# A four-layer graph network: the norm, ranks and feed-forward products of layer 0 inside its attention pass, and the end loops of layers 1 and 3 joined

## The chip, the cores and the metric

One core of a Trainium2 chip runs the whole network in one launch. Times are device microseconds. The time of the kernel before is the median of three runs; its profile comes from one further execution that the hardware profiler recorded. TensorE is called PE (PEld for its weight loads), VectorE DVE, ScalarE ACT, GpSimd POOL, and the queue that issues most plain DMAs SP.

## The reference, cut to what matters

N = 3750 nodes of 256 features, 60000 edges sorted by destination, where destinations are drawn as 3750 u² and so crowd at low node numbers. Eight blocks are added to a residual stream, each on a layer-normed copy:

```python
x = x + L0_gnn(layernorm(x)); x = x + L0_ffn(layernorm(x))   # and so for layers 1, 2, 3
# L0_gnn: relational graph attention, 4 heads, softmax over the edges of each destination
e     = leaky_relu(el[src, type] + er[dst, type], 0.2)
alpha = exp(e - segment_max(e, dst)[dst]);  alpha /= segment_sum(alpha, dst)[dst]
h     = segment_sum(alpha * feat[type, src], dst) + h_bias
# L0_ffn on the normed x: only the N//2 - 1 nodes with the largest router weight get the product
w     = x @ wr + br
sel   = top_k(w, N // 2)[: N // 2 - 1]
out   = x;  out[sel] += w[sel] * (gelu(x[sel] @ w1 + b1) @ w2 + b2)
# L1_ffn: two of 8 experts, chosen from the mean over all nodes
out   = layernorm(sum_of_two_experts(x) + x) * gamma + beta
# L3_ffn: each node goes to two of 16 experts
out   = layernorm(x + moe(x)) * gamma + beta
```

Layers 1 and 2 have attention over the same edges, layer 3 two hypergraph convolutions; layer 2's feed-forward sends each node to one of 8 experts.

## The kernel before

Nodes lie on 128 partitions in NT = 30 tiles, and `self.x` keeps all of them in SBUF. Edges are cut into chunks of 128; each chunk belongs to one destination tile. The list `CAPS` says how many chunks a tile gets (90 for tile 0, 38 for tile 1, down to 10, and 3 for the last), 525 with padding.

**The attention pass** (`Regular.attention`) is one function for layers 0, 1 and 2. It handles GC = 7 chunks as a group, 75 groups in all, and, with 4 heads, NG = 4 groups as a batch for the softmax. Per group g:
- `fetch` issues seven indirect DMA gathers on POOL (L135) into a buffer `gt` of the pool `atg` (9 buffers);
- `choose` makes the transposed one-hot `ohT` of the destinations on ACT (L1780, L1781) and multiplies it on PE into the destination's logit part (`er_ps`, L931);
- `make_logits` adds both parts on DVE (L938 to L943); once a batch, `softmax_1` and `softmax_2` turn logits into weights (DVE scans, an Exp on ACT, transposes on PE);
- four groups later `onehot` makes the one-hot `oh` on ACT (L1789, L1791), `scale_rows` multiplies the gathered rows on DVE (L1897) and copies the weights beside them on ACT (L1898), and `sums` has PE add them up into `sum_ps` (L1915);
- `add` moves finished sums to an accumulator for all tiles, on ACT (L1934) for a tile's first piece and on DVE (L1939, L1940) for those that join.

The pass runs under a manual schedule: on DVE, PE, ACT and POOL the order is that of the Python code. Elsewhere a planner orders the instructions by priority and its own costs. [...]

**Around it.** `l01` runs `l0_gnn`, `l0_ffn`, `l1_gnn`, `l1_ffn`. Behind the gathers of layer 0 it puts 320, and behind those of layer 1 another 160, indirect scatters on POOL (L141): they write a table that later layers read. A memset on DVE at the end of the pass (`behind`) holds them back until the last gathers are out.

`l0_gnn` ends with a loop over the 30 tiles (L952 to L955) that divides, adds the bias and adds to `self.x`. `l0_ffn` then takes statistics of all tiles, transposes all normed tiles to `xT_all`, computes the router row for all nodes (L1014, L1015), and ranks each node against all others: per tile two long compare-and-count operations on DVE over the nodes before it and after it (L1029, L1032). Only with all ranks there do the products start, three tiles at a time: 8 hidden products with Gelu (L1047, L1049), then 24 matmuls for the outputs (L132), then three DVE operations a tile. `l1_gnn` begins with statistics of `self.x` and per tile a product that writes the table its gathers read.

`l1_ffn` has the same loop of threes, keeps all outputs in `f1_y`, and then `add_normed` (L977 to L979) normalises the 30 tiles and adds them to `self.x`; `l2_gnn` takes statistics of `self.x` again. `l3_ffn` runs 74 chunks through their experts, then for each tile norms `self.x` (L118), adds the expert bias (L1759), gathers its two rows by POOL and adds them (L1763), and after all tiles calls `add_normed`; `store` writes the result at the very end.

Of the kernel before, what the change touches and what calls it, by code (L numbers as in the profile page):

```python
# [10 lines left out]
F32 = mybir.dt.float32  # L11
# [10 lines left out]
P = 128  # L22
# [36 lines left out]
class Gnn:  # L59
# [55 lines left out]

    def normed(self, out, src, stats, t):
        mv, rstd = stats
        self.nc.vector.tensor_scalar(out, src[:, t, :], mv[:, t, 0:1], rstd[:, t:t + 1],  # L118
                                     op0=ALU.subtract, op1=ALU.mult)
# [64 lines left out]
    def store(self):  # L184
        nc, out = self.nc, self.out
        for a in range(0, NT - 1, 10):
            b = min(a + 10, NT - 1)
            nc.sync.dma_start(out[a * P:b * P].rearrange("(t p) d -> p t d", p=P), self.x[:, a:b, :])
        nc.sync.dma_start(out[(NT - 1) * P:N], self.x[:NLAST, NT - 1, :])
# [799 lines left out]
    def l0_ffn(self):  # L989
# [3 lines left out]
        with ExitStack() as st:  # L993
# [10 lines left out]
            wm = pool.tile([P, NT], F32, name="f0_wm")  # L1004
            with ExitStack() as st2:
                rp, wp, pp = self.pools(st2, f0r=1, f0rw=2, f0rp=-2)

                wrb = rp.tile([P, 2, P], F32, name="wrb")
                nc.vector.tensor_copy(wrb, wr.to_broadcast([P, 2, P]))
                row = rp.tile([P, NP], F32, name="wrow")  # L1010
                for c0 in range(0, NP, 480):
                    ps = pp.tile([P, 480], F32, name="wr_ps")
# [3 lines left out]
                nc.vector.memset(row[:, N:], -3.0e38)  # L1016

                col = rp.tile([P, NT], F32, name="wcol")
                parts = rp.tile([P, NT, 4], F32, name="rank_parts")
                nc.vector.memset(parts, 0.0)  # L1020
                for t in range(NT):
                    own = row[:, t * P:(t + 1) * P]
                    mask = wp.tile([P, P], F32, name="mask")
                    nc.vector.tensor_tensor(mask, own, self.ident, ALU.mult)
                    nc.vector.tensor_reduce(col[:, t:t + 1], mask, AX.X, ALU.add)
                    w = col[:, t:t + 1]
                    junk = wp.tile([P, NP], F32, name="junk")
                    if t:
                        nc.vector.tensor_scalar(junk[:, :t * P], row[:, :t * P], w, None, op0=ALU.is_ge,  # L1029
                                                op1=ALU.add, accum_out=parts[:, t, 0:1])  # L1030
                    if t < NT - 1:
                        nc.vector.tensor_scalar(junk[:, (t + 1) * P:], row[:, (t + 1) * P:], w, None,  # L1032
                                                op0=ALU.is_gt, op1=ALU.add, accum_out=parts[:, t, 1:2])
                    nc.vector.tensor_scalar(mask, own, w, None, op0=ALU.is_gt, op1=ALU.add,
                                            accum_out=parts[:, t, 2:3])
                    nc.vector.scalar_tensor_tensor(mask, own, w, self.after, op0=ALU.is_equal, op1=ALU.mult,
                                                   accum_out=parts[:, t, 3:4])
                rank = rp.tile([P, NT], F32, name="rank")
                nc.vector.tensor_reduce(rank, parts, AX.X, ALU.add)
                nc.vector.scalar_tensor_tensor(wm, rank, float(KEEP), col, op0=ALU.is_lt, op1=ALU.mult)  # L1040
            wp, pp, yp = self.pools(st, f0w=2, f0p=-3, f0y=-3)
            for t0 in range(0, NT, T):
                hT = wp.tile([P, FC, T * P], F32, name="hT")
                for f in range(FC):
# [4 lines left out]
                    nc.scalar.activation(hT[:, f, :], ps, AF.Gelu_apprx_tanh, bias=b1[:, f:f + 1], scale=1.0)  # L1049
                for t in range(t0, t0 + T):  # L1050
# [716 lines left out]
class Regular(Gnn):  # L1767
# [26 lines left out]
    def attention(self, acc, table, idx, row, W, H, select, logits, with_max=False):  # L1794
# [7 lines left out]
        with ExitStack() as st:  # L1802
# [102 lines left out]
            def sums(g, oh):  # L1905
# [3 lines left out]
                for j in range(GC):  # L1909
# [6 lines left out]
                    if starts(k + 1):  # L1916
                        ready.append(open_)
# [344 lines left out]
```

## Time and profile before

| | us |
|---|---|
| median of three runs | 6599.66 (6581.83 to 6659.76) |
| the profiled execution | 5979.16 |
| its span | 5977.2 |
| layer 0's first gather | 371.3 |
| layer 0's last gather, start | 1031.6 |
| layer 0's ranks (DVE) | 1141 to 1284 |
| layer 0's products (PE) | 1288 to 1494 |
| layer 1's first gather | 1563.4 |
| layer 1's products (PE) | 2355 to 2564 |
| layer 2's first products | 2620.9 |
| layer 3's rows gathered | 5840 to 5915 |
| last DVE operation | 5968 |

Over the span PE is busy 75%, PEld 55%, DVE 51%, ACT 34%, POOL 49%; the mean granted PE clock is 0.828. Numbers such as 0.95 are a duration in us; in the timeline a row is: start, duration, engine, line, operation, output and input, how many merged, and in brackets the idle time before it and what ended it. In the table of waits a row is: who waited, for whom, total us, times, longest.

### The profile page before, as it was taken

What the parts mean: (1) busy time and instruction counts of PE and PEld (TensorE: products, weight loads), DVE (VectorE), ACT (ScalarE), POOL (GpSimd) and SP (SyncE); (2) the same over time, 40 slices, a digit from 0 to 9 for tenths busy, and PEclk for the clock granted to TensorE, in tenths of its full rate; (3) what the DMA queues carried; (4) which work ended last, traced back from release to release, by engine and by line L of the source; (5) the groups of instructions that cost most, each with busy time, mean ns of one, the idle gap of its engine ahead of it and who ended that gap; (6) DMA issues with size and microseconds to landing.
All of it is one profiled execution on the core that took longest, in us unless ns stands there. A gap on an engine that the chain in (4) does not pass through costs nothing.

```text
span 5977.2 us, 64725 instructions
## 1 busy us (share of the span) xinstructions
PE 4455.3 (75%) x20324; PEld 3263.5 (55%) x20438; DVE 3077.3 (51%) x7318; ACT 2042.3 (34%) x4826; POOL 2912.3 (49%) x2845
## 2 busy tenths in 40 slices
PE   5937777239577774967877835997799999995993
PEld 2426666127456652734666623774466666664781
DVE  5454544862343347255888886006533433565336
ACT  1225665112366662213555532223531211110220
POOL 0047777877677778604666610102055546540113
PEclk9967787669777786988888865995599999997995
DMA  4335555100455542015777722223445545554122
GB/s 145 135 112 139 139 141 124 22 1 2 112 140 140 140 116 45 2 53 186 229 222 224 224 79 77 92 74 115 156 150 167 144 128 172 151 127 134 55 56 83
DMA packets 427052, 710.10 MB, mean 119 GB/s; under 512 B 117180, under 2 KB 304516, under 8 KB 422604
## 3 DMA queue, kind: packets, MB, share of 16 engines
q0 software_dynamic: 145136, 379.81, 24.6%
q1 hardware_dynamic: 262952, 312.54, 16.4%
q10 hardware_dynamic: 18612, 13.50, 0.8%
q8 instruction: 166, 2.72, 0.2%
q14 instruction: 186, 1.52, 0.1%
HBM read 579.88 MB, written 125.15 MB: 118 GB/s over the span
## 4 chain that ended last, share of the span: by engine, by line
PE 45%; DVE 14%; issue 6%; DMA 6%; POOL 6%; ACT 3%; DVEq 0%; ACTq 0%; SPq 0%; POOLq 0%
PE third_ps L2136 7%; PE sum_ps L1915 6%; PE y_ps L132 6%; POOL gt L135 5%; PE two_ps L2134 4%; PE hT_ps L1735 3%; PE db_psT L2048 2%; PE y_ps L1744 2%; PE h_ps L1530 2%; PE q_ps L1286 2%; DMA gt<-l_vk,srci 2%; PE qkvs_ps L132 2%; PE h_ps L1232 2%; PE h_ps L1047 2%; DMA gt<-l_h,srci 2%
## 5 line engine op out<-in xcount | busy, mean ns | idle before, releaser
L1915 PE MATMUL sum_ps<-gt,oh 128*128 128x260 f32 (+2 forms) x3150 | 1002.0, 484 | 269.1 <-ACT gt L1898 156.6
L1915 PEld LDWEIGHTS sum_ps<-gt,oh 128*128 128x128 f32 x3150 | 755.5, 246 | 446.3 <-ACT gt L1898 164.6
L135 POOL DMA_INDIRECT gt<-l_vk,srci x525 | 497.9, 948 | 452.8 <-DVE hd_hc L687 231.1
L141 POOL DMA_INDIRECT blocks<-put x480 | 639.7, 1333 | 154.0 <-issue 145.6
L135 POOL DMA_INDIRECT gt<-l_feat,g x525 | 501.5, 955 | 172.8 <-issue 149.0
L135 POOL DMA_INDIRECT gt<-l_h,srci x525 | 496.9, 946 | 178.6 <-issue 138.9
L1789 ACT ACTIVATE oh<-iota,dloc 128x128 f32<-128x128 f32 x1575 | 481.2, 386 | 3.8 <-PE sum_ps L1915 3.8
L1897 DVE TENSOR_TENSOR gt<-gt,bank 128x1792 f32<-128x1792 f32 x225 | 453.5, 2016 | 42.9 <-PE bank L1926 40.0
L135 POOL DMA_INDIRECT gt<-l_mtab,l_idxm x300 | 297.1, 990 | 308.8 <-ACT gt L2120 160.3
L135 POOL DMA_INDIRECT gt<-l_xtab,srci x262 | 254.2, 970 | 321.5 <-DMA l_xtab<-xt 191.9
L132 PE MATMUL y_ps<-f_w,hT 128*128 128x256 f32 x1600 | 351.7, 380 | 0.0
L2134 PE MATMUL two_ps<-l_twom,slab 128*128 128x512 bf16 x1020 | 341.9, 379 | 0.0
L2134 PEld LDWEIGHTS <-slab 128*128 128x128 bf16 x2160 | 211.2, 98 | 235.9 <-issue 0.4
L2134 PE MATMUL two_ps<-l_twox,slab 128*128 128x512 bf16 x1026 | 338.7, 379 | 0.1
L132 PEld LDWEIGHTS y_ps<-f_w,hT 128*128 128x128 f32 x1600 | 304.3, 190 | 46.5
L2136 PE MATMUL third_ps<-l_thirdm,slab 128*128 128x257 bf16 x1080 | 294.8, 273 | 3.2
L2136 PE MATMUL third_ps<-l_thirdx,slab 128*128 128x257 bf16 x1080 | 293.2, 273 | 3.0
L1780 ACT ACTIVATE ohT<-rows,iota_p 128x896 f32<-128x896 bf16 x225 | 235.3, 1046 | 120.6 <-DMA rows<-dl_dram 64.4
L2136 PE MATMUL third_ps<-gt,oh 128*128 128x257 f32 x1124 | 266.3, 382 | 3.3 <-DMA gt<-l_xtab,srci 3.3
L1286 PE MATMUL q_ps<-l_qt,ohT 128*128 128x256 f32 x1050 | 248.8, 390 | 20.1 <-DVE gt L1292 11.9
L125 PE MATMUL xT_ps<-ident,xn 128*128 128x128 f32 x360 | 64.0, 296 | 261.5 <-DVE xn L118 138.4
L1781 ACT ACTIVATE ohT<-ohT,ones 128x896 f32<-128x896 f32 x225 | 234.4, 1042 | 7.3
(541 smaller groups left out, 8463.7 us busy)
## 6 DMA issues: line engine op xcount, KB each, us to landing
rows<-dl_dram SPq DMA_DIRECT2D x225, 224.0 KB
slab<-adT SPq DMA_DIRECT2D x36, 960.0 KB
slab<-ad SPq DMA_DIRECT2D x30, 1152.0 KB
l_feat<-ft SPq DMA_DIRECT2D x30, 1040.0 KB
f_w<-in_L_ffn_w_dram SPq DMA_DIRECT2D x18, 1024.0 KB
adT<-db_rowT SPq DMA_DIRECT2D x36, 480.0 KB
ad<-db_row SPq DMA_DIRECT2D x36, 480.0 KB
f_yt<-y SPq DMA_DIRECT2D x114, 128.0 KB
```

The source lines that it names most:

```text
L132: self.nc.tensor.matmul(ps, xT[:, c, :], w[:, c, :], start=(c == 0), stop=(c == kc - 1))
L135: return self.nc.gpsimd.indirect_dma_start(out=out, out_offset=None, in_=table, in_offset=bass.IndirectOffsetOnAxis(ap=idx, axis=0))
L141: inst = self.nc.gpsimd.indirect_dma_start(out=table, out_offset=bass.IndirectOffsetOnAxis(ap=idx, axis=0), in_=src, in_offset=None)
L1286: nc.tensor.matmul(ps[:, j, :], ohT[:, j * P:(j + 1) * P], flat(q[:, ds(tiles[j], 1), :]), start=True, stop=True)
L1735: nc.tensor.matmul(ps[:, f, :], mine[:, c, f * P:(f + 1) * P], xT[:, c, :], start=(c == 0), stop=(c == 1))
L1780: nc.scalar.activation(t, rows, AF.Abs, bias=self.iota_p, scale=-1.0)
L1781: nc.scalar.activation(t, t, AF.Relu, bias=self.ones[:, 0:1], scale=-1.0)
L1789: nc.scalar.activation(oh[:, j, :], self.iota, AF.Abs, bias=self.dloc[:, c + j:c + j + 1], scale=-1.0)
L1897: nc.vector.tensor_tensor(rows, rows, wj.unsqueeze(3).to_broadcast([P, GC, H, DH]), ALU.mult)
L1915: nc.tensor.matmul(open_[1], oh[:, j, :], gt[:, j, :W], start=starts(k), stop=starts(k + 1))
L2134: nc.tensor.matmul(flat(ps), block, flat(two[n][:, blocks[i][1]]), start=(i == 0), stop=(i == len(blocks) - 1))
L2136: nc.tensor.matmul(ps3[:, :D + 1], block, rhs, start=(i == 0), stop=(i == len(all3) - 1))
```

## The change

**Layer 0.** `l0_gnn` and `l0_ffn` of the regular path become one function, `l0`. `attention` gets two hooks: `done(t, sums)`, called from `add` when tile t has all its sums, which are then taken straight from PSUM or from a small buffer `ring` and no longer kept for all tiles; and `steps(n)`, called twice in each iteration, before `softmax_2` and after `sums`. `done` divides, adds, and takes the statistics of the tile; each pair of tiles then goes through three queues of small pieces. `steps` takes one piece of `nodes` (norm, transpose, router row) per call, one of `ranks` in every fourth call, and one (first call) or two (second) of `products`: 8 hidden products of 256 columns and 4 half outputs per pair. Ranks compare a tile with the tiles before it only; the reverse counts come from matmuls of the bf16 comparison with a column of ones. Outputs go to DRAM unweighted, and after the pass they are read back and added with weight or zero. What is left in the queues is worked off after the pass, behind the issue of the scatters. The pass has 8 gather buffers for 9 and three sum banks for four; products share one PSUM bank `hbank`, router and transposes another, er and the reverse counts a third.

**Layers 1 and 3.** Statistics of `self.x` are taken tile by tile where it is last written. `l1_ffn` norms and adds in its loop of three tiles. `l3_ffn` reads the normed rows from DRAM, where they already are, adds `beta` to `self.x` beside the expert products, and norms, adds and stores three tiles at a time. (The irregular path, which these inputs don't take, has its ranks moved into its product loop.)

```diff
@@ Regular.attention
             def add():
-                k, ps = ready.pop(0)
+                nonlocal ring
+                k, ps, end = ready.pop(0)
                 t = TILE_OF[k]
...
+                last = end == len(TILE_OF) or not joins(end)
+                if joins(k):
+                    out = acc[:, t, :] if done is None else ring
...
+                elif done is None or not last:
+                    out = ring = acc[:, t, :] if done is None else wp.tile([P, W], F32, name="ring")
+                    nc.scalar.copy(out, ps)
+                else:
+                    out = ps
+                if done is not None and last:
+                    done(t, out)
...
                 elif g + 1 == ALL and self.behind is not None:
                     self.behind()
+                steps(0)
                 if new:
                     softmax_2(full)
...
                     sums(k, oh)
+                steps(1)
                 while g >= ALL + NG and ready:
                     add()
@@ Regular.l0
+                def done(t, sums):
...
+                    self.row_stats(mv, bn, self.x, t)
+                    if t % T == T - 1:
+                        two = slice(t + 1 - T, t + 1)
+                        nc.scalar.activation(rstd[:, two], mv[:, two, 1], AF.Sqrt, bias=self.eps, scale=1.0)
+                        nodes.append((norm, t + 1 - T))
+
+                def norm(t0):
+                    nc.vector.reciprocal(rstd[:, t0:t0 + T], rstd[:, t0:t0 + T])
+                    xT = wp.tile([P, 2, T * P], F32, name="xT")
+                    then = []
+                    for i in range(T):
+                        xn = wp.tile([P, D], F32, name="xn")
+                        self.normed(xn, self.x, (mv, rstd), t0 + i)
+                        nc.vector.tensor_tensor(self.x[:, t0 + i, :], self.x[:, t0 + i, :], xn, ALU.add)
+                        then.append((turn, t0 + i, xn, xT))
+                    nodes[:0] = then + [(weigh, t0 + i, xT) for i in range(T)]
+
+                def turn(t, xn, xT):
+                    ps = ybank[:, t % 2 * D:][:, :D].rearrange("p (c n) -> p c n", c=2)
+                    for c in range(2):
+                        nc.tensor.transpose(ps[:, c, :], xn[:, c * P:(c + 1) * P], self.ident)
+                    nc.scalar.copy(xT[:, :, t % T * P:(t % T + 1) * P], ps)
+                    if t % T == T - 1:
+                        products.extend((hidden, xT, f) for f in range(FC))
+                        products.extend((outer, t + 1 - T + i, c) for i in range(T) for c in range(2))
...
+                def compare(t):
...
+                    for i, lo in enumerate(range(0, t * P, HALF)):
+                        hi = min(lo + HALF, t * P)
+                        nc.vector.tensor_scalar(ge[:, :hi - lo], row[:, lo:hi], w, None, op0=ALU.is_ge,
+                                                op1=ALU.add, accum_out=rank[:, t, 2 + i:3 + i])
+                        a, b = lo // P, hi // P
+                        ps = ebank[:, 2 * GC * RH + 32:2 * GC * RH + 32 + b - a]
+                        for u in range(a, b):
+                            nc.tensor.matmul(ps[:, u - a:u - a + 1], ge[:, (u - a) * P:(u - a + 1) * P], one,
+                                             start=True, stop=True)
+                        nc.vector.tensor_tensor(less[:, a:b], less[:, a:b], ps, ALU.add)
+
+                def hidden(xT, f):
...
+                    ps = hbank[:, f % 2 * T * P:(f % 2 + 1) * T * P]
+                    for c in range(2):
+                        nc.tensor.matmul(ps, w1[:, c, f * P:(f + 1) * P], xT[:, c, :], start=(c == 0), stop=(c == 1))
+                    nc.scalar.activation(hT[:, f, :], ps, AF.Gelu_apprx_tanh, bias=b1[:, f:f + 1], scale=1.0)
+
+                def outer(t, c):
+                    ps = hbank[:, t % 2 * D:][:, :D]
+                    for f in range(c * FC // 2, (c + 1) * FC // 2):
+                        nc.tensor.matmul(ps, hT[:, f, t % T * P:(t % T + 1) * P], w2[:, f, :],
+                                         start=(f == 0), stop=(f == FC - 1))
+                    if c:
+                        y = wp.tile([P, D], F32, name="y")
+                        nc.vector.tensor_tensor(y, ps, b2, ALU.add)
+                        nc.sync.dma_start(ydram[t * P:(t + 1) * P], y)
+
+                def do(queue):
+                    if queue and not (queue is nodes and queue[0][0] is norm and len(products) > 2 * T + FC):
+                        f, *args = queue.pop(0)
+                        f(*args)
+
+                def steps(n):
+                    do(nodes)
+                    if next(every):
+                        do(ranks)
+                    for _ in range(1 + n):
+                        do(products)
+                self.attention(None, self.feat, g0, D + H, D + H, H, select, logits, bufs=8, sums_bufs=3,
+                               done=done, steps=steps)
+            behind()
+            while nodes or ranks or products:
+                for queue in (nodes, ranks, products, products):
+                    do(queue)
...
+            for t0 in range(0, NT, G):
+                y = gp.tile([P, G, D], F32, name="f0_got")
+                nc.sync.dma_start(y, ydram[t0 * P:(t0 + G) * P].rearrange("(t p) d -> p t d", p=P))
+                for t in range(t0, t0 + G):
+                    nc.vector.scalar_tensor_tensor(self.x[:, t, :], y[:, t - t0, :], wm[:, t:t + 1], self.x[:, t, :],
+                                                   op0=ALU.mult, op1=ALU.add)
+                    bn = wp.tile([P, 6], F32, name="bn")
+                    self.row_stats(xmv, bn, self.x, t)
@@ l1_ffn
-                        nc.vector.tensor_tensor(y[:, t, :], xn, ps, ALU.add)
-            self.add_normed(pool, y, "L1_ffn_gamma", "L1_ffn_beta", "f1n")
+                        nc.vector.tensor_tensor(y[:, t - t0, :], xn, ps, ALU.add)
+                        self.row_stats(ymv, bn, y, t - t0)
+                    self.inverse_std(yr, ymv)
+                    for t in range(t0, t0 + T):
+                        row, x = y[:, t - t0, :], self.x[:, t, :]
+                        nc.vector.tensor_tensor(x, x, beta, ALU.add)
+                        nc.vector.scalar_tensor_tensor(row, row, ymv[:, t - t0, 0:1], gamma, op0=ALU.subtract, op1=ALU.mult)
+                        nc.vector.scalar_tensor_tensor(x, row, yr[:, t - t0:t - t0 + 1], x, op0=ALU.mult, op1=ALU.add)
+                        self.row_stats(mv, bn, self.x, t)
@@ l3_ffn
-            self.add_normed(yp, y, "L3_ffn_gamma", "L3_ffn_beta", "f3n")
...
+            for t0 in range(0, NT, T):
+                y = wp.tile([P, T, D], F32, name="f3_yall")
+                nc.sync.dma_start(y, xtab[t0 * P:(t0 + T) * P].rearrange("(t p) d -> p t d", p=P))
...
+                        nc.vector.scalar_tensor_tensor(row, r, wts[i][:, t:t + 1], row, op0=ALU.mult, op1=ALU.add)
+                    bn = wp.tile([P, 6], F32, name="bn")
+                    self.row_stats(mv, bn, y, t - t0)
+                self.inverse_std(rstd, mv)
+                for t in range(t0, t0 + T):
+                    row, x = y[:, t - t0, :], self.x[:, t, :]
+                    nc.vector.scalar_tensor_tensor(row, row, mv[:, t - t0, 0:1], gamma, op0=ALU.subtract, op1=ALU.mult)
+                    nc.vector.scalar_tensor_tensor(x, row, rstd[:, t - t0:t - t0 + 1], x, op0=ALU.mult, op1=ALU.add)
+                self.store(t0, t0 + T)
```

## The prediction

> **What bounds the kernel now.** I split the span into stages first (stretches with each engine's busy time, in this order: us, then PE, PEld, DVE, ACT, POOL with instruction counts, granted clock, DMA share, GB/s):
>
> ```profile
> 371.00:1032.00 661.00, 466.03 (x2126) 396.96 (x2127) 315.53 (x687) 392.76 (x847) 501.02 (x525) 0.77 0.55 138
> ...
> 1141.00:1288.00 147.00, 3.78 (x12) 1.90 (x10) 145.94 (x252) 1.77 (x3) 116.84 (x100) 0.52 0.08 1
> 1288.00:1494.00 206.00, 205.86 (x788) 151.09 (x788) 49.45 (x115) 45.80 (x80) 163.87 (x139) 0.98 0.08 2
> ...
> 2565.00:2621.00 56.00, 1.21 (x5) 0.84 (x5) 54.80 (x190) 1.18 (x4) 0.00 (x0) 0.52 0.10 28
> ...
> 5915.00:5977.00 62.00, 0.00 (x0) 0.00 (x0) 53.38 (x184) 0.32 (x1) 0.04 (x1) 0.50 0.20 65
> ```
>
> The first is layer 0's attention pass, then layer 0's ranks (DVE alone) and its feed-forward products (PE alone); the fourth is layer 1's normalisation after its products and the last the end of layer 3 (DVE alone in both). At first sight the 353 us of rows two and three are what the change could hide. The POOL timeline says otherwise:
>
> ```profile
> 1031.56 0.95 POOL L135 DMA_INDIRECT gt<-l_feat,g  x1 [0.30 <-issue]
> 1037.13 1.24 POOL L1997 DMA_DIRECT2D put<-put_dram  x1 [4.62 <-DVE put L1995]
> 1043.22 1.25 POOL L141 DMA_INDIRECT blocks<-put  x1 [4.86 <-DMA put<-put_dram]
> ...
> 1073.48 26.20 POOL L141 DMA_INDIRECT blocks<-put  x1 [0.30 <-issue]
> ...
> 1563.40 0.99 POOL L135 DMA_INDIRECT gt<-l_h,srci  x1 [18.95 <-ACT ohT L1780]
> ```
>
> POOL issues its last layer-0 gather at 1031.6, then 320 scatters until 1544.5, and layer 1's first gather at 1563.4. So ranks and products lie beside scatters that layer 1's gathers queue behind anyway: only 19 us separate the two. In the pass POOL is the bound: a gather every 1.25 us, 7 x 1.25 = 8.75 us per group. Who waits in the pass (us 450 to 1000; total, times, longest), and below it ACT's own timeline:
>
> ```profile
> DVE l L942 <- DMA gt<-l_feat,g: 192.6, 57, 6.5
> POOL gt L135 <- issue: 124.0, 407, 0.3
> ```
>
> ```profile
> 827.88 1.04 ACT L1780 ACTIVATE ohT<-rows,iota_p 128x896 f32<-128x896 bf16 x1
> 828.96 1.04 ACT L1781 ACTIVATE ohT<-ohT,ones 128x896 f32<-128x896 f32 x1
> 829.90 2.14 ACT L1789 ACTIVATE oh<-iota,dloc 128x128 f32<-128x128 f32 x7
> 832.07 1.04 ACT L1791 ACTIVATE oh<-oh,ones 128x896 f32<-128x896 f32 x1
> ...
> 848.34 0.16 ACT L1898 COPY gt<-bank 128x28 f32<-128x28 f32 x1
> ...
> 853.83 0.16 ACT L1898 COPY gt<-bank 128x28 f32<-128x28 f32 x1
> ```
>
> Everything waits for gathers, POOL for nothing. Where gathers are already there, one group's copy (L1898) follows the last by 5.5 us, which is ACT's own work: the compute side has 3.2 us to spare per group, but in a fixed order.
>
> [...]14 sum records take 3.31 us at 821.6 and 5.95 us at 848.6. [...] The trace has loads of 1.28[...].
>
> **Layer 0's pass, part by part.** Removed behind it: finishing (31 us), statistics, transposes, ranks (147), products (206). Added inside: per pair of tiles 5 node steps, 2 comparisons, 8 hidden products, 4 outer ones. Prices: 24 matmuls of 256 columns take 10.36 us (L132), 0.43 each, so a hidden product h is 0.86 and half an outer one o 1.73. A Gelu over 256 columns g: between 0.37 (128 columns, L1741) and 0.58 (384, L1049), I take 0.45. Two transposes 0.5 and their copy 0.37 (L125, L126). Sums s 3.1, er products r 1.65, ohT 2.08, oh 3.2, copy 0.18.
>
> Totals would fit: on DVE a tile adds about 6.3 us (three adds 1.0, bn 0.4, norm and add 0.7, comparison about 1.0 plus 2.3 for the long one, the rest 0.9), 3 us a group beside 315/75 = 4.2. On PE 8 x 0.86 + 4 x 1.73 = 13.8 us a pair. The order doesn't fit. In an iteration ACT does ohT, the Gelu of the product in steps(0), oh, the copy, and then the Gelus of steps(1); these wait for products that PE does after the sums, which wait for the copy. Behind the waiting Gelus stand the next ohT and oh; for them wait er, its logits, and the next sums. So from copy to copy is a closed chain through PE and ACT, which the kernel before doesn't have. By kind of iteration, as the queues fall out when CAPS is worked through (4 iterations a pair once saturated):
> - outer, then turn: s + 2o + r + 0.5 + 0.37 + oh + copy = 12.4
> - turn, then hidden: s + 0.5 + 0.37 + 2h + g + ohT + r + h + g + oh + copy = 14.6
> - hidden, then hidden: the same without the turn, 13.7
> - hidden, then outer: s + 2h + g + ohT + (r + o) + copy = 10.9
>
> Mean 12.9. [...] Rank matmuls, one per earlier tile, some 14 on average by then at the 98 ns of a bf16 weight load (L2134), in every second iteration: 0.7. Table loads between Exp, Gelu and Sqrt mostly fall into ACT's waits, as the one at 393.7 did (Exp followed only at 423.2): 0.1, from 0 up to 1.3 (four in four iterations). Sum 14.3, or 5.55 above POOL's 8.75.
>
> Tiles end late: 90, 38, 30 chunks first, 10 to 15 at the end. Pairs 0 to 2 make bursts (iterations 24 to 41) worth 4, 4.5 and 4 such iterations; from 42 on every one carries products, and POOL's last fetch needs iteration 70: 29. Lag: 22 minus three free iterations that catch up 3.25 each gives 12; plus 25 minus one free one is 34; plus 22 is 56; plus 29 x 5.55 = 161 is 217. POOL's 8 buffers let it stay 3 iterations (26 us) ahead. The last gather is **191 us later**. Bounds: 0 below, since POOL's 1.25 us per gather is untouched and excludes a gain; above, with PE at half clock throughout, the 8 us of PE work in a mean chain (s, r, h, o, transposes) double in 29 + 14 iterations: 191 + 43 x 8 = 535. I take warm PE.
>
> Then the 320 scatters, 320 x 1.484 = 475, 12 before them[...]: layer 1's first gather comes 497 us after the last of layer 0, not 532: **-35**. What remains (10 iterations 143, some 40 products 50, the combine from DRAM 30 x 0.8 = 24 and its loads, layer 1's node products 62) is 290 us and hidden; without scatters it would be the next bound. Layer 1's first statistics (17) vanish there too, worth nothing. SP: 2.1 MB of weights go ahead of the pass's first rows, seg and ends loads; at the 224 GB/s of layer 2's pass 9 us, caught up before iteration 24. The y stores and reloads (3.9 MB each way) meet DMA at a 0.55 share: nothing. toh in bf16: nothing. Three sum banks for four: POOL-bound groups leave them free; 0 to 10, I take 0.
>
> **Layer 1.** Products end at 2564.4, the next layer's first at 2620.9. What remains of it: last tile's add and statistics 1, Sqrt with a load 1.6, three tiles x (add 0.34, two at 0.40, bn 0.39) 4.6, statistics over all tiles 1, norm and transpose 2; per block two table loads on ACT can hold PE (three banks of 1.29 us against 2.9 us of loads and Sqrt) by up to 0.8, ten times 8. 2564 + 10 + 8 = 2583: **-38** (0 to -50). DVE's extra 3.4 us per tile fits: it is busy 51 of the products' 210 us now.
>
> **Layer 3.** POOL's 60 gathers (5840 to 5915) stay. DVE per tile: add 0.34, four fused ones at 0.40, bn 0.39 = 2.35, under POOL's 2.5. After the last gather lands, 5918, some 6 us of arithmetic and the store, 8 as now: 5932 for 5977: **-45**, say -44[...]. The beta adds go beside expert products (DVE busy 157 of 400 us there): nothing.
>
> **Sum.** 191 - 35 - 38 - 44 = +74. The profiled execution took 5979.2 (span 5977.2): 6053. The runs shown have a median of 6599.7, 1.104 times that, for a reason the profile doesn't hold; scaled, +82: **6681**.
>
> **Rivals.**
> - Absorbed: Gelus come early enough, POOL stays the bound, 30 us later. For it: every engine's total fits. Against: the closed chain. 30 - 117 = -87, scaled -96: 6504; beyond 2% only with next to no delay.
> - Slower: PE keeps the pass's clock of 0.77 to 0.78 because ACT still makes it pause. For it: pauses of 2 to 3 us at each ohT and oh; 74% busy already gives only 0.77. Against: layer 2's pass, 81% busy, has 0.86. 8 us of PE per chain become 10.3, 43 x 2.3 = 99 more: +173, scaled +191: 6791. It crosses 2% at a clock of 0.89 (1 us per iteration).
> - The loops of layers 1 and 3 don't pay (ACT's Sqrt holds the Gelus[...]): 60 us less gain, +134, 6748.
>
> **Chances.** The forecast (delay 100 to 234 us, 6581 to 6732) 0.45; absorbed 0.20, half of it beyond 2%; half-warm PE 0.30; loops that don't pay 0.05. So faster by over 2% (about what a measurement of this kernel can tell from no change) 0.10, within 0.55, slower 0.35. Range 6500 (absorbed) to 6830 (half-warm PE with some loads unhidden); the forecast's own 6581 to 6732.
>
> **What will show it.** Right: the last l_feat gather near 1220, ACT waiting for hidden products, copies 13 to 15 us apart in the second half, layer 1's first gather some 497 us later, 18 us between layer 1's products and the next layer, and no bare DVE stretch at the end. Wrong: copies still 8.75 apart (absorbed), or a clock under 0.85 there (slower). What would also upset it: a first gather of layer 1 that waits for its table rather than for scatters.

## The result, and the profile after

The changed kernel takes 6889.4 us (median of four runs, 6872.7 to 6904.3) where the kernel before takes 6590.7 on the same chip: ratio **1.043**, 95% interval 1.035 to 1.051. It is slower, by 299 us instead of the forecast 82.

To read the numbers: on some chips the kernel before takes about 5970 us and on others 6580 to 6720, so every ratio below is against the kernel before on the same chip, and "quick" and "slow" name these two kinds of chip. The profile on which I predicted is from a quick one; the first profile of the changed kernel was from a slow one. Two later executions on a quick chip gave 6315.6 us against 5972.3, ratio 1.058 (1.055 to 1.061): +343 us where my sum, before scaling, said +74. The profile of one of these is shown here, since it compares stage by stage. In it the stages of the attention pass, of what follows it, and of the ends of layers 1 and 3 read (us, then PE, PEld, DVE, ACT, POOL with counts, clock, DMA share, GB/s):

```profile
371.00:1454.00 1083.00, 723.96 (x2969) 582.22 (x2970) 432.97 (x1099) 472.42 (x956) 498.26 (x525) 0.73 0.33 87
1454.00:1998.00 544.00, 210.53 (x1028) 159.85 (x1027) 163.34 (x490) 94.69 (x236) 381.00 (x323) 0.68 0.15 26
2998.00:3009.00 11.00, 2.94 (x11) 1.72 (x11) 8.24 (x24) 1.73 (x5) 0.00 (x0) 0.64 0.35 88
6251.00:6314.00 63.00, 27.46 (x54) 11.01 (x54) 52.73 (x162) 6.95 (x26) 39.63 (x39) 0.50 0.53 163
```

POOL works its 498 us of gathers, as before, but in 1083 us instead of 661; no engine is busy for more than 67% of that. POOL's timeline around the end of the pass:

```profile
1453.47 0.94 POOL L151 DMA_INDIRECT gt<-l_feat,g  x1 [0.30 <-issue]
1515.01 1.24 POOL L2063 DMA_DIRECT2D put<-put_dram  x1 [60.60 <-issue]
1521.13 1.25 POOL L157 DMA_INDIRECT blocks<-put  x1 [4.88 <-DMA put<-put_dram]
...
1997.53 1.00 POOL L151 DMA_INDIRECT gt<-l_h,srci  x1 [0.30 <-issue]
```

The whole difference of the two spans (6313.4 - 5977.2 = 336) lies in four places:

| stage, quick chips | before | after | difference | forecast |
|---|---|---|---|---|
| layer 0's first to last gather | 660.2 | 1081.7 | +421.5 | +191 |
| from there to layer 1's first gather | 531.8 | 544.0 | +12 | -35 |
| layer 1's last to layer 2's first gather | 524.9 | 477.8 | -47 | -38 |
| layer 3's first back gather to the end | 137.3 | 89.6 | -48 | -44 |

The rest adds up to -3. Who waits in the pass (us 450 to 1400; total, times, longest):

```profile
POOL gt L151 <- issue: 425.7, 413, 17.8
ACT hT L2222 <- PE f_hb L2221: 273.8, 64, 11.7
DVE f_row L2189 <- PE f_yb L2187: 186.8, 19, 18.2
PEld sum_ps L1970 <- ACT gt L1953: 136.3, 45, 4.5
...
DVE f_less L2213 <- PE f_eb L2211: 92.3, 19, 15.9
```

ACT waits for hidden products, PE for the copy behind ACT's one-hots: the closed chain of the forecast is there. It is 20.3 us long (copies of groups 42 to 70), not 14.3. One full iteration of it, copy to copy, on ACT and on PE:

```profile
1255.41 0.16 ACT L1953 COPY gt<-bank 128x28 f32<-128x28 f32 x1
1266.95 0.47 ACT L2222 ACTIVATE hT<-f_hb,f_b 128x256 f32<-128x256 f32 x1 [11.38 <-PE f_hb L2221]
1269.59 0.47 ACT L2222 ACTIVATE hT<-f_hb,f_b 128x256 f32<-128x256 f32 x1 [2.17 <-PE f_hb L2221]
...
1277.22 0.47 ACT L2222 ACTIVATE hT<-f_hb,f_b 128x256 f32<-128x256 f32 x1 [5.15 <-PE f_hb L2221]
1277.59 2.14 ACT L1840 ACTIVATE oh<-iota,dloc 128x128 f32<-128x128 f32 x7
1279.76 1.04 ACT L1842 ACTIVATE oh<-oh,ones 128x896 f32<-128x896 f32 x1
1280.71 0.16 ACT L1953 COPY gt<-bank 128x28 f32<-128x28 f32 x1
```

```profile
1255.63 5.58 PE L1970 MATMUL sum_ps<-gt,oh 128*128 128x260 f32 x14 [3.74 <-ACT gt L1953]
1261.05 0.61 PE L2187 MATMUL f_yb<-xT,f_wrb 128*128 128x128 f32 x4
1265.44 0.50 PE L2211 MATMUL f_eb<-f_one,f_ge 128*128 128x1 bf16 x14 [3.79 <-DVE f_ge L2206]
1265.80 1.11 PE L2221 MATMUL f_hb<-xT,f_w 128*128 128x256 f32 x4
1267.48 2.08 PE L2221 MATMUL f_hb<-xT,f_w 128*128 128x256 f32 x4 [0.56 <-ACT hT L2222]
1272.12 3.19 PE L2126 MATMUL f_eb<-l_er,ohT 128*128 128x32 f32 x14 [2.57 <-ACT ohT L1832]
1275.13 2.05 PE L2221 MATMUL f_hb<-xT,f_w 128*128 128x256 f32 x4
```

ACT does nothing for 11.4 us after the copy. What PE does in that time is the comparison of the section on the prediction. The `ohT` that stands behind two of the Gelus in the written order (L1831) starts at 1269.96, right behind the second one.

### The profile page after: what moved, and what is told of

It is laid out like the page before. It is cut to its first block, busy times and chain, and to the rows that moved or that the text cites. A ratio compares the mean times of both kernels' runs of the same rounds, so it can differ in the third digit from the quotient of the medians.

```text
span 6884.0 us, 66326 instructions
## 1 busy us (share of the span) xinstructions
PE 4705.1 (68%) x21121; PEld 3421.0 (50%) x21121; DVE 3025.6 (44%) x7328; ACT 2132.8 (31%) x4948; POOL 2889.3 (42%) x2845
## 5 line engine op out<-in xcount | busy, mean ns | idle before, releaser
L1970 PE MATMUL sum_ps<-gt,oh 128*128 128x260 f32 (+2 forms) x3150 | 1041.1, 494 | 418.8 <-ACT gt L1953 205.7
L157 POOL DMA_INDIRECT blocks<-put x480 | 619.1, 1290 | 154.2 <-issue 145.7
L2400 PE MATMUL two_ps<-l_twox,slab 128*128 128x512 bf16 x1080 | 370.8, 391 | 22.2 <-issue 22.1
L1130 PE MATMUL ad_ps<-l_node,ohT 128*128 128x4 f32 x1050 | 148.7, 265 | 323.3 <-DVE l L1137 259.2
L1831 ACT ACTIVATE ohT<-rows,iota_p 128x896 f32<-128x896 bf16 x225 | 234.5, 1042 | 426.7 <-issue 258.1
L2400 PE MATMUL two_ps<-l_twom,slab 128*128 128x512 bf16 x1080 | 359.8, 379 | 0.0
L1130 PEld LDWEIGHTS ad_ps<-l_node,ohT 128*128 128x128 f32 x1050 | 155.2, 223 | 323.0 <-issue 318.3
L2126 PE MATMUL f_eb<-l_er,ohT 128*128 128x32 f32 x1050 | 185.4, 341 | 190.4 <-issue 71.2
L2126 PEld LDWEIGHTS f_eb<-l_er,ohT 128*128 128x128 f32 x1050 | 180.6, 265 | 207.3 <-issue 139.7
```

Of the source, the lines that this page charges most:

```text
L157: inst = self.nc.gpsimd.indirect_dma_start(out=table, out_offset=bass.IndirectOffsetOnAxis(ap=idx, axis=0), in_=src, in_offset=None)
L1130: nc.tensor.matmul(ps[:, j, :], ohT[:, j * P:(j + 1) * P], node[:, ds(tiles[j], 1), :H].rearrange("p a h -> p (a h)"), start=True, stop=True)
L1831: nc.scalar.activation(t, rows, AF.Abs, bias=self.iota_p, scale=-1.0)
L1970: nc.tensor.matmul(open_[1], oh[:, j, :], gt[:, j, :W], start=starts(k), stop=starts(k + 1))
L2126: nc.tensor.matmul(ps[:, j, :], ohT[:, j * P:(j + 1) * P], flat(er[:, ds(tiles[j], 1), :]), start=True, stop=True)
L2400: nc.tensor.matmul(flat(ps), block, flat(two[n][:, blocks[i][1]]), start=(i == 0), stop=(i == len(blocks) - 1))
```

## Experiments

**1. The kernel before again** (no edit).

> The kernel before once more, for a profile of an execution like its timed ones: the profile shown took 5979 us, its timed runs about 6590. If the missing 600 us are spread evenly over the network, layer 1's pass (first to last gather, 656 us in the profile shown) takes about 790, as it does in the profile of the changed kernel, with idle time of some us on POOL that no other engine's work ends; if the profile shown was right and the timed runs lose time elsewhere, the pass takes 656 again. Span: 6590 or 5980.

Span 6655.9 on a slow chip. Layer 0's gathers take 808 us, layer 1's 790, as I had expected, and POOL's timeline shows where the time goes:

```profile
896.71 0.95 POOL L135 DMA_INDIRECT gt<-l_feat,g  x1 [0.30 <-issue]
901.06 0.95 POOL L135 DMA_INDIRECT gt<-l_feat,g  x1 [3.40 <-issue]
```

A pause of 3.4 us for which the trace shows no releaser, absent from the quick profile (the longest wait of this kind in its pass is 0.3). From the tenth group on there are 34 pauses of over 1 us, each in front of the first gather of a group, 157 us together; the pass is 148 us longer. It is still POOL's, at 10.7 us a group. So on slow chips 808 is the pass to compare with.

**2. The changed kernel on two more chips** (no edit).

> The changed kernel once more, for chips of both kinds: on one chip the kernel before took 5970 us, as in the profile shown before the change, on the others 6580 to 6720. If this run falls on a quick chip: my sum gives a pass of 661 + 191 = 852 us and 6053 in all, ratio 1.014. If the terms that the slow chips' trace showed too small (sums and er at a half clock, PE waiting 3.8 us for the comparisons, the second hidden product behind the first one's Gelu) hold there as well, the cycle in the second half is about 18 us, the pass 950 to 1050 us, ratio 1.03 to 1.045. On a slow chip: pass 1180 and ratio 1.043 as before.

> The changed kernel on one more chip, for the question that after_again left (its chip took 6590 us for the kernel before). On a chip of the quick kind: by my sum pass 852 us, ratio 1.014; with the mis-sized terms of the closed chain pass 950 to 1050 us, ratio 1.03 to 1.045. On a slow chip pass about 1180, ratio 1.043 to 1.05.

after_again: slow chip, pass 1182, ratio 1.048 (1.046 to 1.050). after_third: quick chip, pass 1082, ratio 1.058, shown above. That is over both of my expectations for a quick chip: even with the mis-sized terms I had said 950 to 1050 us and 1.03 to 1.045. The added 376 us (1184 - 808) of a slow chip and 421 of a quick one are the change's own: the forecast did not fail because of the chip. Groups 42 to 70 take 20.4 us each on the slow chip and 20.3 on the quick one; a chain through PE, ACT and DVE hides POOL's pauses.

**3. The pieces out of the pass.** First by leaving their place to the planner, then by holding them behind the pass in the written order.

```diff
# products_after
-                self.attention(None, self.feat, g0, D + H, D + H, H, select, logits, bufs=8, sums_bufs=3,
-                               done=done, steps=steps)
+                self.attention(None, self.feat, g0, D + H, D + H, H, select, logits, bufs=8, sums_bufs=3,
+                               done=done)
# products_last: as well, attention() gets a hook called after its loop, inside the written order
+            tail()      # while nodes or ranks or products: one piece of each, two of products
```

> As the changed kernel, but no piece of the three queues is worked off in the attention pass: norm, ranks and products of all 15 pairs follow it, beside the scatters. Finishing and statistics of a tile stay in the pass. Theory of the closed chain (the delay is made by the products inside the pass): first to last layer-0 gather as in the kernel before (about 661 us in its quick profile, up to 740 in a usual one), layer 1's first gather at most 540 us after the last of layer 0, and the whole kernel faster than before by 90 to 130 us, ratio 0.98 (0.975 to 0.99). If instead finishing tiles in the pass, the three sum banks or the eight gather buffers are what slowed it, the pass stays over 900 us and the ratio over 1.0.

> As the changed kernel, but all pieces of the three queues are now held behind the pass by the written order (in products_after the planner had moved 82 of the 120 Gelus back into it). Finishing and statistics of a tile stay in the pass, beside its 8 gather buffers and 3 sum banks. If the pieces alone make the delay, the pass takes 800 to 830 us as in the kernel before (808) and layer 1's first gather follows the last of layer 0 by 505 us instead of 551: ratio to the kernel before 0.975 to 0.985. If finishing tiles in the pass, the buffers or the banks cost something, the pass is longer by just that.

products_after: ratio 1.002 (0.998 to 1.005), pass 935. The planner put pieces back into the pass: 51 of 120 Gelus ran before the last gather (the second expectation says 82, a miscount). Its placement costs 127 us against the 376 of the written one. products_last: **pass 805 us**, as before the change; finishing tiles, 8 buffers and 3 banks cost nothing, the pieces cost everything. But the ratio is 1.005 (1.003 to 1.007), not 0.98, since my other expectation failed:

```profile
1669.72 1.18 POOL L157 DMA_INDIRECT blocks<-put  x1 [0.30 <-issue]
1824.36 1.00 POOL L151 DMA_INDIRECT gt<-l_h,srci  x1 [153.46 <-PE ad_ps L1130]
```

Without the pass to hide in, the same small pieces and layer 1's table outlast the scatters by 153 us; layer 1's first gather comes 648 us after the last of layer 0, against 551 for the loops of the kernel before.

**4. Single terms of the chain.**

```diff
# ranks_last: comparisons only in the hook behind the pass
-                    if next(every):
-                        do(ranks)
# two_banks: hbank and hbank2, sums_bufs=2
-                    ps = hbank[:, f % 2 * T * P:(f % 2 + 1) * T * P]
+                    ps = (hbank2 if f % 2 else hbank)[:, :T * P]
# warm: zeros added to an open sum ahead of its real matmuls
+                if done is not None and not starts(g * GC):
+                    for _ in range(12):
+                        nc.tensor.matmul(open_[1][:, :32], self.zero, self.ident[:, :32], start=False, stop=False)
```

> As the changed kernel, but the comparisons of ranks are worked off behind the pass; norm, router and products stay in it. Theory: PE waits 3.8 us for each comparison of DVE (at 1359.8 to 1363.6 of the changed kernel), with a hidden product and so ACT's Gelu and one-hots queued behind it; two of these per pair, shorter for early tiles. Without them the pass shortens by 60 to 110 us from 1184, ratio to the kernel before 1.027 to 1.035. Rival (comparisons fall into waits that are there anyway): pass within 20 us of 1184, ratio 1.04.

> As the changed kernel, but the two halves of hbank are two PSUM banks, and the sums have two banks instead of three. In the changed kernel the second of two hidden products starts only when the first one's Gelu is over (0.56 us after it, then ACT waits 1.22 us): three such pairs of hidden products per pair of tiles. Theory: with two banks it starts at once; 1 us less for each, some 3 us of the 84 us of a pair, pass 20 to 50 us shorter, ratio 1.035 to 1.04. Rival: nothing gained, or the third sum bank was needed and the pass gets longer.

> As the changed kernel, plus 12 small matmuls of zeros (128x32) ahead of the sums of a group where a sum goes on, so that PE has something to do while it waits 3.75 us for the copy. Theory (PE's half clock is part of the loss): sums that follow take 3.1 to 3.5 us instead of 4.8 to 5.9, the granted clock in the pass rises above 0.80 from 0.73, and the pass shortens by 40 to 90 us. Rival (the half clock is a symptom and the fillers only add work): the pass stays or lengthens by up to 60 us.

ranks_last: pass 1144 (-40), ratio 1.038 (1.036 to 1.040): comparisons in the pass do cost time, but less than my 60 to 110. two_banks: pass 1156 (-28), 1.0395 (1.031 to 1.048). It also takes away a sum bank, and its times can't be told from the changed kernel's 1.043 (1.035 to 1.051), so the 28 us rest on one profile; two profiles of one kernel lie up to 12 us apart (late_all and late_all2 below). warm: pass 1234 (**+50**), 1.057 (1.055 to 1.058). The rival won there; PE's timeline in it:

```profile
1414.23 2.05 PE L2226 MATMUL f_hb<-xT,f_w 128*128 128x256 f32 x4
1416.08 5.17 PE L1966 MATMUL sum_ps<-ident,f_zero 128*128 128x32 f32 x24
1421.06 5.77 PE L1973 MATMUL sum_ps<-gt,oh 128*128 128x260 f32 x14
```

The fillers themselves ran slowly (5.17 us for 24 records; 2.8 by my estimate from the quick pace of the er products, 14 records in 1.64), overran the copy by 1.1 us and left the sums at 5.77. The clock in the second half was 0.74 against 0.73. Filling one of an iteration's pauses did not warm PE; so the share of the slow clock alone was not isolated.

**5. The same work, in another order.** late_gelu puts each Gelu and each copy of a transposed tile one call of `steps` later on ACT, and the first call behind the one-hots. late_all does the same with DVE's reading of router and outer products, and leaves comparisons to the hook behind the pass. late_bf16 is late_all with bf16 operands in the products (their results are rounded).

```diff
# late_gelu
+                def emit():              # first thing in steps()
+                    while late:
+                        late.pop(0)()
-                    nc.scalar.activation(hT[:, f, :], ps, AF.Gelu_apprx_tanh, bias=b1[:, f:f + 1], scale=1.0)
+                    late.append(lambda: nc.scalar.activation(out, ps, AF.Gelu_apprx_tanh, bias=b1[:, f:f + 1], scale=1.0))
# late_all, as well
+                    late.append(row_out)     # row <- ps + br, then ranks.append
+                        late.append(y_out)   # y <- ps + b2, store
# late_bf16, as well
-                        hT = hp.tile([P, FC, T * P], F32, name="hT")
+                        hT = hp.tile([P, FC, T * P], BF16, name="hT")
```

> All the work of the changed kernel in the pass, but each Gelu and each copy of a transposed tile stands on ACT one call of the steps later than its matmuls, and the first call comes behind the one-hots; so ACT no longer waits for a product just begun. Closed-chain theory: ACT's waits for hidden products (245 us between 800 and 1550 in the changed kernel) fall below 60, the pass shrinks from 1184 us to 750 to 850, ratio to the kernel before 0.98 to 1.0. Rival (the sum of PE's work at a half clock and DVE's waits for the router and the counts set the time, not ACT's order): the pass stays above 1050 us, ratio 1.03 or more.

> As late_gelu, and also DVE takes the results of router and outer products one call of the steps later, and the comparisons of ranks are worked off behind the pass. No engine then waits in the pass for a piece that another has just begun. Closed-chain theory: of the 258 us that late_gelu's pass (1066) still has over the kernel before (808), 120 to 200 go: pass 870 to 950, ratio to the kernel before 0.99 to 1.01. Rival (what is left is the sum of work at PE's half clock and the stalls of single engines): pass over 1000, ratio over 1.015.

> The kernel of late_all once more, beside after_again on the same chip. On a quick chip, if the closed chain is the loss there too, its pass is 100 to 200 us shorter than that of after_again and the ratio to the kernel before 0.995 to 1.01; on a slow chip pass 945 and 1.0067 as before.

> As late_all, but weights, inputs and Gelus of layer 0's products are bf16, so that one of their matmuls takes a fraction of the 0.43 us of a 32-bit one; one more copy of 0.37 us per tile on ACT. The products are rounded to bf16. late_all's pass (945 us) is 140 over that of the kernel before. If that is PE's load, the pass falls to 830 to 880 and the ratio below 1.0 (0.985 to 0.998). If it is the order of the remaining pieces and single stalls, the pass stays above 910 and the ratio at 1.0 or more.

| kernel, slow chips | pass | ratio (95%) |
|---|---|---|
| changed | 1184 | 1.043 (1.035 to 1.051) |
| changed, again | 1182 | 1.048 (1.046 to 1.050) |
| late_gelu | 1066 | 1.027 (1.018 to 1.037) |
| late_all | 945 | 1.0067 (1.0044 to 1.0089) |
| late_all2 | 933 | 1.0049 (1.0026 to 1.0072) |
| late_bf16 | 901 | 1.0020 (0.9985 to 1.0054) |
| before | 808 | 1 |

Order, with the comparisons behind the pass, takes 239 of the 376 us away in late_all and 249 in late_all2 (933 against after_again's 1182 on the same chip); the comparisons alone were 40. In late_gelu ACT's waits for hidden products fell from 245 us to 51, as I had said, but the pass is on the rival's side of 1050: 118 us came back, not the 330 or more that I had expected. One thing that still stood in the way was DVE behind products (its outputs' add waited 87 us in us 450 to 1400). In late_all PE runs at its quick pace more often: in groups 42 to 70 the 14 records of a group's sums have a median of 3.8 us, against 5.0 in the changed kernel. PE's timeline of late_all, where two groups follow each other without ACT in between:

```profile
1116.51 1.64 PE L2129 MATMUL f_eb<-l_er,ohT 128*128 128x32 f32 x14
1117.99 0.69 PE L2200 MATMUL f_yb<-xT,f_wrb 128*128 128x128 f32 x4
1118.52 1.03 PE L2236 MATMUL f_hb<-xT,f_w 128*128 128x256 f32 x4
1119.39 3.28 PE L1970 MATMUL sum_ps<-gt,oh 128*128 128x260 f32 x14
```

er 1.64, a hidden product 1.03 and sums 3.28: the prices of my forecast. late_bf16, where a hidden product takes 0.38 us (at 1108.91), takes another 32 to 44 us off, less than the 65 I set as its least if PE's load were the rest; its pass of 901 lies between my two forecasts. Its sums are slow again (median 4.8 us), and still its pass is the shortest of those with the pieces in it. 93 us over 808 stay unexplained.

**6. What pays.** loops_only has layer 0 of the kernel before with the loops of layers 1 and 3, and takes layer 1's statistics where layer 0's outputs are added. finish_early adds only `done` (divide, add, statistics in the pass).

```diff
# finish_early, in l0_gnn (its loop over 30 tiles is gone)
-                self.attention(acc, feat, g0, D + H, D + H, H, select, logits)
+                self.attention(None, feat, g0, D + H, D + H, H, select, logits, done=done)
+            self.inverse_std(rstd, mv)       # l0_ffn takes these statistics
```

> Layer 0 as in the kernel before; only the loops of layers 1 and 3 are those of the changed kernel. My theory (they gain 38 + 44 us of the quick profile): about 90 us faster than the kernel before, ratio 0.986 (0.98 to 0.99). The rival that they don't pay: ratio 0.995 to 1.005. If they cost time: above 1.005.

> Once more only the loops of layers 1 and 3, on the same chip as finish_early2: 0.9895 with an interval of 0.98 to 0.9995 before; from the profiles (48 us between layer 1's last gather and layer 2's first, 45 after layer 3's gathers begin) 90 us, ratio 0.986 (0.983 to 0.991).

> The kernel before with the loops of layers 1 and 3 of the changed kernel, and of layer 0 only the hook that finishes a tile in the pass (divide, bias, add, statistics); norm, ranks and products follow the pass as in the kernel before, under the planner. Finishing in the pass was free in products_last (pass 805), and without the run of adds the scatters took 475 us instead of 503. So pass 800 to 815, layer 1's first gather 505 to 520 us after the last of layer 0 (541 in loops_only): 20 to 40 us under loops_only, ratio to the kernel before 0.983 (0.978 to 0.988), the fastest. If what follows the pass, and not the scatters, sets layer 1's first gather, it comes at 535 or later and the ratio is 0.988 or more.

> The same kernel as finish_early, whose times had no interval (one execution took 18246 us, the others 6523 to 6632). In its profile the pass took 806 us, the scatters 476 and layer 1's first gather came 511 us after the last of layer 0, 30 us sooner than in loops_only: ratio to the kernel before 0.983 (0.978 to 0.988), 20 to 40 us under loops_only on the same chip. If the profile's 30 us don't show in the times, both ratios agree within 0.003.

loops_only: 0.9895 (0.980 to 0.9995) and, on a quick chip (loops_only2), **0.983** (0.982 to 0.985): 99 us. Some 10 of them come before layer 1's first gather, which follows the last of layer 0 after 522 us instead of 532. finish_early's four times give no interval (one execution took 18246 us); finish_early2, on the chip of loops_only2, gives **0.978** (0.977 to 0.980), 5842.1 us against 5871.5 and 5970.4 before. It is faster than the kernel before and than the changed one. Its scatters take 475 us (502 in loops_only2) and the next gather follows at once:

```profile
1519.12 1.17 POOL L157 DMA_INDIRECT blocks<-put  x1 [0.30 <-issue]
1520.59 1.00 POOL L151 DMA_INDIRECT gt<-l_h,srci  x1 [0.30 <-issue]
```

## Why the prediction was wrong

The closed chain was there, and the loops of layers 1 and 3 gave 95 us where I had 82. The step that failed is **the sum over the four kinds of iteration, 14.3 us: it measured 20.3**. (The 14.3 are 12.9 for the mean of the four, 0.7, 0.1, and 0.6 for results on their way from PE to ACT, an estimate of mine with no row behind it: the Gelu at 1266.95 starts 0.04 us after the end of its product.) An estimate with 20.3 in my own sum (12.5 iterations before group 42, 29 after it, three iterations of lead) makes the last gather 405 us late instead of 191, and 421.5 were measured. So this term is some 214 of the 230 us that the pass missed by; another 47 were missed behind the pass (point 5), where even the direction was wrong. On the quick chip the four iterations from 1198.48 to 1280.71 take 13.4, 21.8, 21.8 and 25.3 us, 82.2 for a pair of tiles, where I had 57.2. The last one, the longest, term by term from the two timelines above, each term from its start to the start of the next:

| hidden, then hidden | forecast | measured |
|---|---|---|
| sums | 3.1 | 5.6, with their start 0.2 after the copy |
| router product | none | 0.6 |
| PE waits for the comparison, then counts | 1.4 (14 matmuls of 98 ns) | 4.1 (3.79 of it idle) |
| two hidden products and a Gelu | 2.2 | 4.2, two Gelus |
| ohT | 2.1 | 2.2 |
| er | 1.65 | 3.0 |
| hidden product, Gelu | 1.3 | 2.5 |
| oh, copy | 3.4 | 3.1 |
| together | 15.2 | 25.3 |

1. **PE's clock.** I took warm PE. Sums, er and three hidden products together take 13.7 us for my 7.3, over half of what this iteration is longer. The slow price of the sums stood in the profile before, which has both (x14 are the records of one group):

```profile
821.63 3.31 PE L1915 MATMUL sum_ps<-gt,oh 128*128 128x260 f32 x14
848.56 5.95 PE L1915 MATMUL sum_ps<-gt,oh 128*128 128x260 f32 x14 [2.54 <-ACT gt L1898]
```

The granted clock is 1.00 during the first (us 821.6 to 824.9) and 0.55 during the second (848.5 to 854.5). Their median over groups 42 to 70 is 4.9 us, hidden behind POOL's 8.75. I had expected the added work to warm PE; in the changed kernel (quick chip) the median is 5.3. The rival "half-warm PE" had named this, at 0.30, and its sign, a clock under 0.85, came true (0.73), but I had priced it with the pass's old 0.77 (2.3 us), so that its +173 us were too few as well; in these four iterations the clock is 0.75, 0.81, 0.66 and 0.63. My argument against it went by shares of busy time: layer 2's pass before has 0.86 at 81% busy (us 2800 to 3463), this pass 0.73 at 67%, with pauses of 3.74 and 3.79 us in this iteration. (My 74% busy and 0.77 came from two stretches: us 450 to 1000 have 74% and 0.79, the whole pass 71% and 0.77.) The pause in front of the sums tells more than such shares. In the kernel before, groups 20 to 73, all 19 sums that begin after a pause of 2.26 us or more take 4.8 to 6.3 us, and of the 35 after a shorter pause or none 24 take 3.2 to 3.4 and 11 take 4.8 to 5.9; in the changed kernel's first profile all 37 after a pause of 2.33 us or more take 4.7 to 6.3. Pauses in a row: those of 6.23 us at 1233.85 (quick chip) follow pauses of 2.45, 0.80 and 2.34 us with about 1 us of work between them. What the clock alone costs stays open: no run isolates it, and late_bf16, with sums of 4.8 us, has a pass 283 us shorter than the changed kernel's.
2. **Work that another engine must do first.** I priced the rank matmuls as 98 ns each. Fourteen of them take 0.50 us; what they cost is the DVE chain in front of them: the router row's add, four operations on the tile, the long comparison of 2.08 us. Hidden product, Gelu and one-hots are queued behind that wait. Without any comparisons the pass is 40 us shorter (ranks_last).
3. **One bank for two halves.** I let the second hidden product run during the first one's Gelu. It started 0.06 us after it. PE was idle for 0.56 us at 1267.48 and released by ACT's Gelu on the first half, though the halves are different addresses of the bank. I had priced the halves as independent. With two banks, and one sum bank fewer, the pass is 28 us shorter.
4. **DVE's place in the chain.** I had worked out ACT's and PE's queues and only DVE's total. In the outer-then-turn kind the softmax of the batch stands on DVE behind the add of an outer product, and ACT's Exp and one-hots behind the softmax:

```profile
1223.92 0.21 DVE L2138 SCALAR_TENSOR_TENSOR lg<-l 128x28 f32<-128x28 f32 x1
1227.26 0.42 DVE L2231 TENSOR_TENSOR y<-f_hb,f_b 128x256 f32<-128x256 f32 x1 [3.12 <-PE f_hb L2227]
1227.60 0.27 DVE L1919 TENSOR_TENSOR y<-bank,ends_b 112x114 f32<-112x114 f32 x1
...
1228.98 0.29 DVE L1926 TENSOR_TENSOR fw<-bank,mc 112x128 f32<-112x128 f32 x1
```

5. **The stage behind the pass.** I gave 12 us between the last gather and the first scatter; it is 68 (1453.47 to 1521.13). I had counted POOL's lead over the rest as a gain of 26 us for the last gather, but the scatters wait for a memset that stands on DVE behind that lead, so the lead is given back and more, as it grew from 26 to 60 us with the longer iterations:

```profile
1513.70 0.59 DVE L2060 MEMSET put<- 125x640 int32 x1
```

The scatters themselves are 25 us shorter. The 497 us that I gave this stage are 475 for them, 12 before them, and 10 that were my estimate for what DVE's operations beside them would still cost; in the kernel before that is 26 (501 us from first scatter to last, less 475), so I had 16.
6. **What held.** The tail is hidden by the scatters: layer 1's gather follows at 1997.5 without waiting for its table. Layers 1 and 3 gave 47 and 48 us for my 38 and 44: the next layer's products begin 11 us after layer 1's, not 18. "The loops don't pay" fell, and so did "absorbed": each engine's total fits (at most 67% busy), and the pass still takes 1082 us.

Scaling by 1.104 was wrong in kind, though small here (8 us): POOL's pauses lengthened the pass that POOL sets (660 to 808 us), while the closed chain took 20.3 and 20.4 us an iteration on the two kinds of chip.

## What to carry to other kernels

When small pieces of other work are put into a pipelined loop, let a result be consumed at least one step after it is produced, on every engine: that order, with the comparisons put behind the pass, gave some 240 of 376 us back here. Price such a chain with every engine's queue written out (DVE too), PE at the slow price that the trace shows behind waits of some microseconds (here sums of 4.7 to 6.3 us behind pauses of 2.3 us or more, for 3.3), and every producer that must finish before an inserted matmul. Test the parts alone: here the unspectacular ones, the two loops with statistics where a tile is last written, and finishing a tile in the pass, are worth 2.2% together, and the large move costs more than they bring.

## What the runs showed of the hardware

- The same kernel takes 5970 us on some chips and 6580 to 6720 on others. On the slow ones POOL pauses, mostly for 3.4 to 4.8 us, in front of the first gather of about every second group, in most cases with nothing in the trace that ends the pause; PE waits without a releaser too (before_again, us 450 to 1150: 67 times in front of its er products, 78.8 us together), and so do ACT (5 times in front of Gelus, 22.1 us) and DVE (5 times in front of the router row's add, 73.7 us) in the changed kernel's profile from a slow chip (us 450 to 1500). Why is open.
- 12 added matmuls ahead of a group's sums, wherever a sum goes on, meant to keep PE warm, cost 50 us and left the clock at 0.74.
- 320 scatters take 501 us in the kernel before and 475 in finish_early2 and in the changed kernel. The difference is one scatter: 26.2 us in the kernel before (28.9 in loops_only2), while in finish_early2 and in the changed kernel none takes over 2 us. The 26.2 us (1073.48 to 1099.68) lie beside DVE's run of two-input operations without a pause (L952 to L955, 1068.4 to 1098.6), which finish_early2 and the changed kernel don't have there. Behind layer 1's pass, where such a run stands in both kernels, one scatter takes 47.3 us (before: 2261.66 to 2308.99, the run from 2258.5 to 2309.3) and 46.7 (the changed kernel's first profile: to 2990.2, the run to 2990.6). Why it ends with the run is not shown.
